# Graph attention on one Trainium2 core: the source-term rows, the maxima, the out-degrees and the second load of x change their places

## The chip, the cores and the metric

The kernel runs on one core of a Trainium2 chip. The metric is the device time of one execution in microseconds (us): from the runs, the median. Five engines work beside each other: TensorE (PE; its weight loads are PEld), VectorE (DVE), ScalarE (ACT), GpSimd (POOL) and SyncE (SP, which only issues transfers here). DMAs are issued by SP and by POOL; each of the two has a queue of its own.

## What is computed

Two layers on 1250 nodes with 1024 features and 20000 edges; each step adds to x. The first step is the graph attention that this change is about:

```python
z = jnp.einsum('ni,hif->nhf', h, W)            # h = layernorm(x); 4 heads of 256
el = jnp.einsum('nhf,hf->nh', z, a_l)
er = jnp.einsum('nhf,hf->nh', z, a_r)
e = jax.nn.leaky_relu(el[src] + er[dst], 0.2)
m = jax.ops.segment_max(e, dst, num_segments=N)
ex = jnp.exp(e - m[dst])
s = jax.ops.segment_sum(ex, dst, num_segments=N)
out = jax.ops.segment_sum((ex / s[dst])[:, :, None] * z[src], dst, num_segments=N)
```

Then follow a feed-forward step (rails, gelu and one large product), a graph convolution, for which the out-degree of each node (plus one, to the power -1/2) is needed, and a mixture of eight experts. Those three are not touched, but for the place where the out-degrees are made.

## The kernel before

The 1250 nodes are ten tiles of 125 (T = 10, R = 125). The edges become a dense matrix of counts: `count(d)` multiplies one-hot matrices of the edges on PE for the destinations of tile d, and `finish` writes the counts to DRAM (`cnt_d`, for the graph convolution), a mask `nm_d` (-1e30 where there is no edge) to DRAM too, and the transposed counts as 16-bit integers to `CT`, which stays in SBUF.

The four heads go in two pairs, g = 0 and 1. `z_weights(g)` loads the weights of a pair; `z_tile(g, t)` multiplies on PE (L131), copies the result to `Z` on ACT (L132), and makes the pair's `el` and `er` of the tile with four VectorE instructions (L136). The counting stage holds all of the first pair's z between the counts (L225 to L240). Then comes a branch (L242, L243): were the edges not sorted as expected, all counts would be made anew. The branch holds every engine, and what lies in it can't be mixed with other work.

Behind the branch, for a pair:

- `maxima(g)` needs `el` of the pair as two rows on all 125 partitions. `to_rows` (L107 to L115) makes them: transpose on PE, copy on ACT (L112), a DMA of 9.8 KB to a row in DRAM (L114) and a second one, 1220.7 KB, that spreads the row to all partitions (L115), both on POOL's queue. Then for each tile d a mask of 125 x 1250 is loaded from `nm_d` on SP's queue (two DMAs, L45 and L46; two buffers), and one VectorE instruction a head (L264) adds mask and row and keeps the maximum: 20 of them for a pair. `maxima` is a generator: it gives control back after each, so that its caller can put other work between.
- `bounds(g)` makes two small tables from the maxima (L272 to L278) and has `to_rows` spread them, one head after the other, as `rows[h]` (two buffers for four heads).
- `attend(h, b)` does head h for half b of the destinations in ten steps: L317 on VectorE, an exponential on ACT (L318), L321 on VectorE (times the counts), five matmuls on PE (L323). Then five results are divided and added to `X` (L327 to L331). So `X`, a second copy of x that collects the sums, must be there at the end of the first pass. u and w have three buffers. After each step it may draw one piece from a generator given to it (`between`).

The order as it is written (L284 to L366): `maxima(0)` is drawn two at a time behind each tile of the second pair's z; bounds(0); the out-degrees `dis` (ten sums over `CT`, L298, then L299 to L301); the second load of x into `X` (ten tiles, two DMAs each, on SP's queue, L305); then, with `maxima(1)` drawn one a step, the passes (0,0), (0,1), (1,0); bounds(1); then (1,1), (2,0), (3,0), (2,1), (3,1).

The program is written with a layer that sets the semaphores and places the buffers. When it builds the program it may move an instruction ahead of others of its engine that are written earlier, if its inputs and its buffer are free. So the file's order is a wish, and the trace shows what became of it: L298 stands behind the first pair's maxima in the file and starts at 246.6 us, while the first maximum starts at 265.4; of the ten tiles of the second pair's z, two are copied out before the branch (at 234.7 and 241.6 us) and eight behind it. A buffer of a pool that reuses another pool's space waits until that is released; the pool `mx0` of the first pair's maxima takes space of the counting stage.

Of the kernel before, what the change touches and what calls it, by code (L numbers as in the profile page):

```python
# [20 lines left out]
R, T = 125, 10  # L21
# [16 lines left out]
def gnn_ffn_kernel(ctx, tc, x, src, dst, gat_w, a_l, a_r, maker, up, cproj,  # L38
# [65 lines left out]
    el, er, mx, el2, el8 = (zp.tile([R, H, T], F32, name=n) for n in ("el", "er", "mx", "el2", "el8"))  # L104
    xT = xTp.tile([P, KD, N], F32, name="xT")

    def to_rows(pool, psp, dst_t, cols, k, n):  # L107

        pt = psp.tile([P, 4, R], F32, name="pt")
        nc.tensor.transpose(pt[:k, 0, :], cols, ident[:R, :R])  # L110
        st = pool.tile([k, R], F32, name=f"st{k}", bufs=1)
        nc.scalar.copy(st, pt[:k, 0, :])  # L112
        row = dram.tile([k, R], F32, name=f"row{n}")
        nc.gpsimd.dma_start(row, st)  # L114
        nc.gpsimd.dma_start(dst_t, row.rearrange("k r -> (k r)").partition_broadcast(R))  # L115

    with tc.tile_pool(name="gw", bufs=1) as gwp, tc.tile_pool(name="gps", bufs=3, space=PSUM) as psp:
# [10 lines left out]
        def z_tile(g, t):  # L128
            pz = psp.tile([R, 2, F], F32, name="pz", bufs=2)
            for k in range(KD):  # L130
                nc.tensor.matmul(pz, xT[:, k, t * R:(t + 1) * R], W[g][:, k], start=(k == 0), stop=(k == KD - 1))  # L131
            nc.scalar.copy(Z[:, t, 2 * g:2 * g + 2, :F], pz)  # L132
            for h in (2 * g, 2 * g + 1):
                for i, e in enumerate((el, er)):
                    sc = gwp.tile([R, F], F32, name="sc", bufs=2)
                    nc.vector.scalar_tensor_tensor(sc, Z[:, t, h, :F], 1.0, aw[g][:, i, h - 2 * g, :], op0=ALU.mult,  # L136
                                                   op1=ALU.mult, accum_out=e[:, h, t:t + 1])

        with tc.tile_pool(name="cc", bufs=1) as ccp, tc.tile_pool(name="cw", bufs=2) as cwp:
# [102 lines left out]
            elsewhere = nc.values_load(flag[0:1, 0:1], min_val=0, max_val=1)  # L242
            with tc.If(elsewhere > 0):  # L243
# [7 lines left out]
                                                 start=(c == 0), stop=(c == EC - 1))  # L251
                        finish(d, pc)

        def maxima(g, mxp, psp):

            el_row = mxp.tile([R, 2, N], F32, name="el_row")
            to_rows(mxp, psp, el_row.rearrange("p a n -> p (a n)"), el[:, 2 * g:2 * g + 2, :].rearrange("p h t -> p (h t)"),
                    2 * T, f"el{g}")
            for d in range(T):
                nm = mxp.tile([R, N], F32, name="nm2", bufs=2)  # L260
                dma(nc.sync, nm, nm_d[d])
                for h in (2 * g, 2 * g + 1):
                    sc = mxp.tile([R, N], F32, name="sc2")
                    nc.vector.tensor_tensor_reduce(sc, nm, el_row[:, h - 2 * g, :], scale=1.0, scalar=-3.0e38,  # L264
                                                   op0=ALU.add, op1=ALU.max, accum_out=mx[:, h, d:d + 1])
                    yield

        def bounds(g, pool, psp, rowp):

            hs = slice(2 * g, 2 * g + 2)  # L270
            for dst_t, f in ((el2, SLOPE), (el8, 1.0 - SLOPE)):
                nc.vector.tensor_scalar(dst_t[:, hs], el[:, hs], f, None, op0=ALU.mult)  # L272
            top = pool.tile([R, 2, T], F32, name="top")
            nc.vector.tensor_tensor(top, mx[:, hs], er[:, hs], op=ALU.add)
            nc.vector.scalar_tensor_tensor(top, top, SLOPE, top, op0=ALU.mult, op1=ALU.max)
            bd = pool.tile([R, 2, 2, T], F32, name="bd")
            nc.vector.tensor_tensor(bd[:, :, 0], er[:, hs], top, op=ALU.subtract)
            nc.vector.scalar_tensor_tensor(bd[:, :, 1], er[:, hs], SLOPE, top, op0=ALU.mult, op1=ALU.subtract)  # L278
            for h in range(2):
                rows[2 * g + h] = rowp.tile([R, 2, N], F32, name="rr", bufs=2)  # L280
                to_rows(pool, psp, rows[2 * g + h].rearrange("p a n -> p (a n)"), bd[:, h].rearrange("p a t -> p (a t)"),
                        2 * T, f"bd{2 * g + h}")

        rows = {}  # L284
        rowst = ExitStack()
        rowp = rowst.enter_context(tc.tile_pool(name="rowp", bufs=1, side="right"))
        with tc.tile_pool(name="mx0", bufs=1) as mxp:
            search = maxima(0, mxp, psp)
            for t in range(T):
                z_tile(1, t)  # L290
                next(search)
                next(search)
            for _ in search:
                pass
            bounds(0, mxp, psp, rowp)

            for t in range(T):
                nc.vector.tensor_reduce(dis[:, t:t + 1], CT[:, t, :], AX.X, ALU.add)  # L298
            nc.vector.tensor_scalar(dis, dis, 1.0, None, op0=ALU.add)  # L299
            nc.scalar.activation(dis, dis, AF.Sqrt)  # L300
            nc.vector.reciprocal(dis, dis)  # L301

    X = ctx.enter_context(tc.tile_pool(name="xpool", bufs=1)).tile([R, T, D], F32, name="X")
    for t in range(T):
        dma(nc.sync, X[:, t, :], x_t[t])  # L305
    HN = N // 2
    HT = T // 2
    norm = {}
    with tc.tile_pool(name="att", bufs=3) as atp, tc.tile_pool(name="aps", bufs=6, space=PSUM) as aps, \
# [21 lines left out]
                nc.vector.scalar_tensor_tensor(xs, po[i][:, :F], rs, xs, op0=ALU.mult, op1=ALU.add)  # L331

        with tc.tile_pool(name="mx1", bufs=1) as mxp:
            search = maxima(1, mxp, tps)
            for h, b in ((0, 0), (0, 1), (1, 0)):
                attend(h, b, search)
            for _ in search:
                pass
            bounds(1, mxp, tps, rowp)
            attend(1, 1)  # L340
        xT = xTp.tile([P, KD, N], F32, name="xT")
        with tc.tile_pool(name="al", bufs=2) as lnp:
            attend(2, 0)
# [517 lines left out]
```

## Time and profile before

| what | value |
|---|---|
| time, median of 3 runs | 3266.51 us (3264.94 to 3267.15) |
| the profiled execution's own time | 3264.68 us |
| its span, first to last instruction | 3263.0 us |
| its mean granted PE clock | 0.987 |
| maxima L264, both pairs | 40, 1.46 us each, from 265.4 to 405.7 us |
| out-degree sums L298 | 10, 1.45 us each, from 246.6 to 279.2 us |
| spread of a source row, second pair | 19.4 us from issue to landing |
| spread of a bounds row | 4, 7.8 to 8.0 us from issue to landing |
| second load of x | 20 DMAs on SP's queue, issued from 322.9 to 350.3 us |
| one attention matmul L323 | 800 records, mean 394 ns |

The profile is of one execution, so places in it are given in us from its first instruction. A busy time is what an engine's instructions took; two neighbouring ones overlap a little, so a row of equal instructions is better counted from start to start. What is named behind an idle time is the event that came last before the engine went on. Transfers are listed with the time from issue to landing. An instruction of a float32 matmul appears as two records.

### The profile page before, as it was taken

What the parts mean: (1) busy time and instruction counts of PE and PEld (TensorE: products, weight loads), DVE (VectorE), ACT (ScalarE), POOL (GpSimd) and SP (SyncE); (2) the same over time, 40 slices, a digit from 0 to 9 for tenths busy, and PEclk for the clock granted to TensorE, in tenths of its full rate; (3) what the DMA queues carried; (4) which work ended last, traced back from release to release, by engine and by line L of the source; (5) the groups of instructions that cost most, each with busy time, mean ns of one, the idle gap of its engine ahead of it and who ended that gap; (6) DMA issues with size and microseconds to landing.
All of it is one profiled execution on the core that took longest, in us unless ns stands there. A gap on an engine that the chain in (4) does not pass through costs nothing. (4 is left out here: it accounts for less than half of the span.)

```text
span 3263.0 us, 23844 instructions
## 1 busy us (share of the span) xinstructions
PE 3159.9 (97%) x9330; PEld 1552.0 (48%) x9330; DVE 1641.6 (50%) x2621; ACT 354.8 (11%) x470; POOL 128.9 (4%) x202
## 2 busy tenths in 40 slices
PE   8996798999999999999999999999999899999998
PEld 5572686444444444444444444444444344445674
DVE  6567897555555555555555555554555720211113
ACT  1211234000000100000010000001000011000000
POOL 1000000000000000000000000000000000001001
PEclk9998898999999999999999999999999999999999
DMA  4245511101110110111011011101110201213564
GB/s 116 59 110 133 146 32 55 39 27 33 39 33 27 40 39 27 33 39 33 27 37 42 27 33 36 37 27 33 40 31 13 77 5 39 70 41 103 182 211 152
DMA packets 104961, 189.76 MB, mean 58 GB/s; under 512 B 32713, under 2 KB 51245, under 8 KB 104088
## 3 DMA queue, kind: packets, MB, share of 16 engines
q1 hardware_dynamic: 95158, 161.26, 16.6%
q0 software_dynamic: 9680, 26.85, 2.9%
q8 instruction: 78, 1.28, 0.2%
q14 instruction: 45, 0.37, 0.0%
HBM read 156.86 MB, written 31.21 MB: 58 GB/s over the span
## 5 line engine op out<-in xcount | busy, mean ns | idle before, releaser
L484 PE MATMUL po<-B,gt 128*125 128x512 f32 x1920 | 836.0, 593 | 0.0
L489 DVE TENSOR_TENSOR acc<-po,acc 125x512 f32<-125x512 f32 x620 | 425.9, 690 | 486.1 <-PE po L484 483.0
L484 PEld LDWEIGHTS po<-B,gt 128*125 128x125 f32 x1920 | 360.7, 188 | 465.0 <-issue 457.0
L484 PE MATMUL po<-t,s 128*125 128x512 f32 x1280 | 559.8, 592 | 0.0
L484 PEld LDWEIGHTS po<-t,s 128*125 128x125 f32 x1280 | 237.9, 188 | 294.1 <-issue 293.6
L495 DVE TENSOR_TENSOR X<-po,X 125x512 f32<-125x512 f32 x320 | 220.8, 690 | 262.3 <-PE po L484 262.3
L484 PE MATMUL po<-B,s 128*125 128x512 f32 x640 | 299.5, 607 | 0.0
L484 PE MATMUL po<-t,gt 128*125 128x512 f32 x640 | 280.4, 592 | 2.8 <-DVE X L493 2.3
L438 ACT ACTIVATE gt<-pz 128x1668 f32<-128x1668 f32 (+1 forms) x96 | 149.8, 1560 | 688.8 <-PE pz L436 688.8
L323 PE MATMUL po<-Z,w 125*125 125x257 f32 x800 | 187.1, 394 | 30.6 <-DVE w L321 16.8
L484 PEld LDWEIGHTS po<-t,gt 128*125 128x125 f32 x640 | 119.9, 188 | 158.0 <-issue 145.9
L484 PEld LDWEIGHTS po<-B,s 128*125 128x125 f32 x640 | 112.5, 187 | 165.4 <-issue 108.9
L323 PEld LDWEIGHTS po<-Z,w 125*125 125x125 f32 x800 | 152.9, 195 | 63.0 <-DVE w L321 29.6
L634 PE MATMUL ph<-Hs,cs 125*125 125x512 f32 x400 | 173.5, 593 | 0.0
L493 DVE TENSOR_TENSOR X<-X,po 125x512 f32<-125x512 f32 x160 | 109.5, 686 | 120.1 <-PE po L484 120.1
L131 PE MATMUL pz<-W,xT 128*125 128x512 f32 x320 | 141.4, 596 | 3.7 <-ACT Z L132 3.7
L574 PE MATMUL ph<-W,xT 128*125 128x512 f32 x320 | 140.1, 596 | 0.0
L427 ACT COPY pw<-pz 128x128 f32<-128x128 f32 x32 | 8.5, 265 | 1131.7 <-PE pz L424 1131.7
L216 PE MATMUL pc<-os,od 125*125 125x417 f16 (+1 forms) x642 | 119.2, 343 | 1.0 <-DVE od L187 1.0
L634 PEld LDWEIGHTS ph<-Hs,cs 125*125 125x125 f32 x400 | 74.3, 188 | 93.1 <-issue 93.1
L665 PE MATMUL pab<-xgT,w 128*128 128x256 f32 x512 | 112.0, 379 | 1.4 <-DVE xgT L762 1.4
L665 PEld LDWEIGHTS pab<-xgT,w 128*128 128x128 f32 x512 | 96.6, 190 | 15.5 <-DVE xgT L762 1.9
(181 smaller groups left out, 2104.3 us busy)
## 6 DMA issues: line engine op xcount, KB each, us to landing
B<-in_cproj SPq DMA_DIRECT2D x128, 512.0 KB, 3.8
w<-in_w SPq DMA_DIRECT2D x16, 1024.0 KB, 8.1
nm<-nm_d SPq DMA_DIRECT2D x20, 546.9 KB, 4.4
w3t<-in_w SPq DMA_DIRECT2D x8, 1024.0 KB, 7.0
ys_d<-y SPq DMA_DIRECT2D x16, 512.0 KB, 5.3
cnt_d<-cn SPq DMA_DIRECT2D x10, 546.9 KB, 6.3
nm_d<-nm SPq DMA_DIRECT2D x10, 546.9 KB, 6.1
cs<-cnt_d SPq DMA_DIRECT2D x10, 546.9 KB, 4.2
```

Source lines behind the costliest of these rows:

```text
L131: nc.tensor.matmul(pz, xT[:, k, t * R:(t + 1) * R], W[g][:, k], start=(k == 0), stop=(k == KD - 1))
L216: nc.tensor.matmul(pc[:, b, :nn], od[:, d - near[c][0], :], os[:, n0:n0 + nn], start=(c == win[d][0]), stop=(c == win[d][-1]))
L323: nc.tensor.matmul(po[i], w[:, i * R:(i + 1) * R], Z[:, s, h, :], start=(s == 0), stop=(s == T - 1))
L427: nc.scalar.copy(pw[b], pp[:, 0, :P])
L438: nc.scalar.activation(gt[b][:, :, n0:n0 + nn], pz[:, :, :nn], AF.Gelu)
L484: nc.tensor.matmul(po, a[:, k, n * R:(n + 1) * R], w[:, k, :], start=(k == 0), stop=(k == 1))
L489: tt(acc[m][:, n, :], po, acc[m][:, n, :], op=ALU.add)
L493: tt(x, x, po, op=ALU.subtract)
L495: tt(x, po, x, op=ALU.add)
L574: nc.tensor.matmul(ph[:, g, :], xT[:, k, t * R:(t + 1) * R], W[:, k, g * 512:(g + 1) * 512], start=(k == 0), stop=(k == KD - 1))
L634: nc.tensor.matmul(pa[:, g, :], cs[:, c, :], Hs[:, c, g * 512:(g + 1) * 512], start=(c == late_first[0]), stop=(c == late_first[-1]))
L665: nc.tensor.matmul(pab[:, :nn], w12[:, i, k, f * P:(f + 1) * P], rhs[:, k, n0:n0 + nn], start=(k == 0), stop=(k == KD - 1))
```

## The change

Several steps are moved; no arithmetic changes.

- `to_rows` is split: `to_row` writes the row to DRAM, `spread` brings it to all partitions. `el_row(g, ...)` is `to_row` for the source terms of a pair.
- The first pair's source row is written ahead of the branch, from a pool of the counting stage; behind it, `maxima(0)` has only to spread it. The masks get three buffers for the first pair (two for the second, as before).
- The first pair's maxima are drawn three at a time ahead of each tile of the second pair's z, so all 20 are drawn by the seventh tile.
- The second load of x goes to POOL's queue, where it stands behind the bounds' rows.
- The second pair's source row is written ahead of the pass (0,0), but spread, and its maxima drawn, only from the pass (0,1) on.
- The out-degrees become a generator, one sum a step, that the pass (1,1) draws.

```diff
-    def to_rows(pool, psp, dst_t, cols, k, n):
+    def to_row(pool, psp, cols, k, n):
...
         row = dram.tile([k, R], F32, name=f"row{n}")
         nc.gpsimd.dma_start(row, st)
+        return row
+
+    def el_row(g, pool, psp):
+        return to_row(pool, psp, el[:, 2 * g:2 * g + 2, :].rearrange("p h t -> p (h t)"), 2 * T, f"el{g}")
+
+    def spread(dst_t, row):
+
         nc.gpsimd.dma_start(dst_t, row.rearrange("k r -> (k r)").partition_broadcast(R))
...
+            row0 = el_row(0, cwp, psp)
 
             elsewhere = nc.values_load(flag[0:1, 0:1], min_val=0, max_val=1)
...
-        def maxima(g, mxp, psp):
+        def maxima(g, mxp, row):
 
-            el_row = mxp.tile([R, 2, N], F32, name="el_row")
-            to_rows(mxp, psp, el_row.rearrange("p a n -> p (a n)"), el[:, 2 * g:2 * g + 2, :].rearrange("p h t -> p (h t)"),
-                    2 * T, f"el{g}")
+            els = mxp.tile([R, 2, N], F32, name="els")
+            spread(els.rearrange("p a n -> p (a n)"), row)
             for d in range(T):
-                nm = mxp.tile([R, N], F32, name="nm2", bufs=2)
+                nm = mxp.tile([R, N], F32, name="nm2", bufs=3 - g)
...
         with tc.tile_pool(name="mx0", bufs=1) as mxp:
-            search = maxima(0, mxp, psp)
+            search = maxima(0, mxp, row0)
             for t in range(T):
+                for _ in range(3):
+                    next(search, None)
                 z_tile(1, t)
-                next(search)
-                next(search)
-            for _ in search:
-                pass
             bounds(0, mxp, psp, rowp)
-
-            for t in range(T):
-                nc.vector.tensor_reduce(dis[:, t:t + 1], CT[:, t, :], AX.X, ALU.add)
-            nc.vector.tensor_scalar(dis, dis, 1.0, None, op0=ALU.add)
-            nc.scalar.activation(dis, dis, AF.Sqrt)
-            nc.vector.reciprocal(dis, dis)
...
     for t in range(T):
-        dma(nc.sync, X[:, t, :], x_t[t])
+        dma(nc.gpsimd, X[:, t, :], x_t[t])
...
-            search = maxima(1, mxp, tps)
-            for h, b in ((0, 0), (0, 1), (1, 0)):
-                attend(h, b, search)
-            for _ in search:
-                pass
+            def degrees():
+
+                for t in range(T):
+                    nc.vector.tensor_reduce(dis[:, t:t + 1], CT[:, t, :], AX.X, ALU.add)
+                    if t == T - 1:
+                        nc.vector.tensor_scalar(dis, dis, 1.0, None, op0=ALU.add)
+                        nc.scalar.activation(dis, dis, AF.Sqrt)
+                        nc.vector.reciprocal(dis, dis)
+                    yield
+
+            row1 = el_row(1, mxp, tps)
+            attend(0, 0)
+            search = maxima(1, mxp, row1)
+            attend(0, 1, search)
+            attend(1, 0, search)
             bounds(1, mxp, tps, rowp)
-            attend(1, 1)
+            attend(1, 1, degrees())
```

More of the change, by code (lines that the diff above doesn't have):

```diff
@@ L263, in maxima @@
                     sc = mxp.tile([R, N], F32, name="sc2")
-                    nc.vector.tensor_tensor_reduce(sc, nm, el_row[:, h - 2 * g, :], scale=1.0, scalar=-3.0e38,
+                    nc.vector.tensor_tensor_reduce(sc, nm, els[:, h - 2 * g, :], scale=1.0, scalar=-3.0e38,
                                                    op0=ALU.add, op1=ALU.max, accum_out=mx[:, h, d:d + 1])
@@ L280, in bounds @@
                 rows[2 * g + h] = rowp.tile([R, 2, N], F32, name="rr", bufs=2)
-                to_rows(pool, psp, rows[2 * g + h].rearrange("p a n -> p (a n)"), bd[:, h].rearrange("p a t -> p (a t)"),
-                        2 * T, f"bd{2 * g + h}")
+                spread(rows[2 * g + h].rearrange("p a n -> p (a n)"),
+                       to_row(pool, psp, bd[:, h].rearrange("p a t -> p (a t)"), 2 * T, f"bd{2 * g + h}"))
         rows = {}
```

## The prediction

> **What bounds the kernel now.** I read the page's busy table first, then the windows around the change, then the timeline inside them.
>
> ```profile
> PE 3159.9 (97%) x9330; PEld 1552.0 (48%) x9330; DVE 1641.6 (50%) x2621; ACT 354.8 (11%) x470; POOL 128.9 (4%) x202
> ```
>
> TensorE (PE) is the bound of the program as a whole, so only its idle time can be won. The windows from the branch (244) to the last attention pass (515) show where that is. Columns: window, its length, then busy time (and instructions) of PE, PEld, DVE, ACT and POOL, granted clock, DMA share, GB/s.
>
> ```profile
> 244.00:258.00 14.00, 13.70 (x34) 5.90 (x33) 9.65 (x14) 1.43 (x3) 1.04 (x2) 1.00 0.76 196
> 258.00:301.00 43.00, 39.27 (x91) 16.65 (x90) 34.40 (x77) 2.93 (x6) 0.00 (x0) 1.00 0.46 124
> 301.00:326.00 25.00, 0.98 (x4) 0.22 (x3) 13.13 (x37) 4.63 (x8) 3.11 (x6) 0.59 0.41 107
> 326.00:420.00 94.00, 76.08 (x303) 60.93 (x304) 82.06 (x143) 25.39 (x33) 0.00 (x0) 0.87 0.51 128
> 420.00:515.00 95.00, 93.39 (x446) 78.86 (x445) 87.22 (x169) 40.76 (x56) 2.07 (x4) 1.00 0.11 27
> ```
>
> PE is idle for 3.7 us in the second, 24.0 in the third, 17.9 in the fourth, 1.6 in the last: with 0.3 in the first some 47 us, all that this change can reach. The timeline says why (start, duration, engine, line; idle before and its releaser in brackets).
>
> ```profile
> 246.61 2.82 DVE L298 TENSOR_REDUCE dis<-CT 125x1 f32<-125x1250 int16 x2 [2.96 <-DVEq L243]
> 247.22 0.51 POOL L114 DMA_DIRECT2D rowel<-st  x1 [74.90 <-ACT st L112]
> 251.84 0.53 POOL L115 DMA_DIRECT2D el_row<-rowel  x1 [4.11 <-DMA rowel<-st]
> 265.44 1.46 DVE L264 CUSTOM_DVE_ANT_0 sc<-nm,el_row 125x1250 f32<-125x1250 f32 x1 [9.19 <-issue]
> ...
> 286.29 0.21 ACT L300 ACTIVATE dis<-dis 125x10 f32<-125x10 f32 x1 [16.11 <-DVE dis L299]
> 287.03 14.00 PE L131 MATMUL pz<-W,xT 128*125 128x512 f32 x32 [3.73 <-ACT Z L132]
> ...
> 310.68 0.25 DVE L272 TENSOR_SCALAR el<-el 125x20 f32<-125x20 f32 x2
> 312.62 0.51 POOL L114 DMA_DIRECT2D rowbd<-st  x1 [60.25 <-ACT st L112]
> 314.49 0.53 POOL L115 DMA_DIRECT2D rr<-rowbd  x1 [1.36 <-DMA rowbd<-st]
> 322.89 2.43 DVE L317 SCALAR_TENSOR_TENSOR u<-rr,el 125x625 f32<-125x625 f32 x3 [11.37 <-DMA rowbd<-st]
> 326.09 10.58 PE L323 MATMUL po<-Z,w 125*125 125x257 f32 x40 [11.10 <-DMA X<-in_x]
> 342.92 1.46 DVE L264 CUSTOM_DVE_ANT_0 sc<-nm,el_row 125x1250 f32<-125x1250 f32 x1 [10.91 <-DMA el_row<-rowel]
> 345.17 16.05 PE L323 MATMUL po<-Z,w 125*125 125x257 f32 x62 [8.49 <-DVE w L321]
> ```
>
> The chain after the branch: row to DRAM, spread to all partitions, 20 maxima from 265.4 to 310.7, bounds, row, spread, 322.9 first attention step, 326.1 first matmul. PE's z product is over at 301. Then the second pair's row arrives at 342.9, after 19.4 us of DMA, and VectorE stands 10.9 us before it with the weights of the next steps queued behind. From there on VectorE is the bound (362 to 420: it is nearly always busy). The order on an engine isn't the file's: L298 is written after all maxima and runs first, L272 of the first pair runs at 176.8, before the branch. Ready instructions are moved up.
>
> [...] a row of 9.8 KB behind a spread on POOL's queue landed after 7.6 us; a spread took 7.8 to 8.0 us alone and 19.4 beside the loads of x on SP's. [...] at 168 to 174 VectorE was busy throughout and POOL's weight loads went out each 0.72 us, with 270 to 337 GB/s moving. [...] clock 0.50 at 314 to 328, and an attention matmul of 0.22 us pitch takes up to 0.79 us there; so each long gap costs about 2 us more.
>
> **The change, part by part.** Durations are of the profiled execution (span 3263.0, time 3264.68); its time is 1.8 us under the median 3266.51, so I add 1.8 at the end.
>
> *Row ahead of the branch.* One PE transpose (0.27), one copy (0.26), one 9.8 KB DMA. All first-pair scores are there at 167.4, so they go into the counting stage; 0.3 us on PE there, 0.3 less behind the branch: nothing. The spread can then be issued with the first load after the branch, at 246.7 instead of 251.8: 5.1 us. It now shares the DMA engines with five tiles of 0.61 MB (three buffers for the first pair, and two that the second pair already fetches now at 248.7) instead of four. At half of the 250 GB/s of that stretch its 1.25 MB need 10 us from 248.5: 259. Bounds: 257[...], 266 if it lands with all 4.3 MB. I take 259, against 265.4 now.
>
> *Maxima ahead of z.* 20 x 1.38 (step to step) = 27.6. Of the eight groups of four score products (4 x 0.345 = 1.38), two come before 259; about four more come before the end of the maxima, 5.5. Waits for nm as now 1.1; the third buffer can take these away. Two out-degree sums caught between, 2.7. End: 259 + 27.6 + 5.5 + 1.1 + 2.7 = 296, against 310.7. The score products behind a waiting maximum hold nobody but the second pair's row: ScalarE's copy L132 frees z's PSUM. From there the same chain as now, 310.7 to 322.9 = 12.2: first step at t0 = 308 instead of 322.9, **15 us earlier**. Bounds: 20 (no sums between, row at 257) and 2 (row at 266, all groups and four sums). The end of z (297 without the 3.7 us that ScalarE's root L300 costs) isn't late then.
>
> *Out-degrees later.* 10 x 1.37 = 13.7 on VectorE, one root, one reciprocal. They read only CT, so nothing ties them to the last pass of this stage; by what L298 does now I expect some five in the wait for the spread row, two as above, the rest in the 11 us wait for the bounds' rows: nothing beyond the 2.7. If they stay where written: an attention pass has 22.0 us of PE and about 18.6 of VectorE (18.2 of 21 and 19.2 of 22 in two quiet windows), cover 3.4, so 10.3 us lost; the root among exponentials adds up to two table loads of 1.28 (as at 322.7) on ScalarE, which is mostly idle. Bounds 0 and 10.3; I take 0.
>
> *Second load of x on POOL's queue.* 20 issues of about 0.53 leave SP, whose nm loads no longer stand behind them, and stand on POOL between the bounds' rows and the second source row. First spread lands at t0, second at t0 + 8, x (5.12 MB at about 250 GB/s) at t0 + 28. The first pass needs half of x at its end, t0 + 27: it landed at about t0 + 18; free. The second source row's spread comes last: t0 + 36. If the 9.8 KB row itself falls behind x, some 3 to 5 more.
>
> *Second pair's maxima from the second pass on.* 27.6 us of VectorE come onto two passes (37.2) instead of three. First pass: 3.2 to first matmul, 22.0, cold clock 2: over at t0 + 27. VectorE has then done three or four steps of the next and waits for t0 + 36, about 9 us (10.9 now). From there 37.2 + 27.6 less 7 done = 58, so the second bounds at about t0 + 92 with the last sums of that pass behind them; now 413.05 - 322.89 = t0 + 90.2. **2 us lost**; bounds: 4 gained if the row doesn't hold it (t0 + 86), 8 lost with a late row.
>
> Sum: 15 - 2 = 13 us. 3264.7 - 13 = 3251.7, with 1.8: **3253**. Everything after 420 shifts as it is.
>
> **The rivals.**
> - *All hidden* (3242): row at 257, no sums between, the second row in time: 20 + 4 = 24. For it: VectorE has idle time to put sums in, as 258 to 265 shows. [...]
> - *Washed out* (3264): 15 is halved to 8 by a late row or sums between the maxima, and the rest goes to the late second row (6 to 8) or to sums that stay in their pass. For it: the 10.9 us wait now; 18.6 + 13.7 is over 22.0.
> - *Slower* (3281): x on POOL's queue is slow. At 150 GB/s it needs 34 us, the row behind it 4 and the spread 8: the second row lands at t0 + 54, 18 later than taken, all of it VectorE wait in the stretch where VectorE is the bound; and the sums, with no gap left, stay in place: 15 - 20 - 10 = -15. It decides from a landing at t0 + 49 on if the sums cost nothing, t0 + 39 if they cost 10. [...] Against: 270 to 337 GB/s of POOL's loads under a busy VectorE.
> - That the order is left as it was can't be excluded, as the builder moves instructions; but row0's buffer is the one thing that held it behind the branch, so this falls under the washed case.
>
> **Numbers.** Likeliest 0.55 (own range 3246 to 3261), all hidden 0.15, washed out 0.17, slower 0.13. About 0.2% (6.5 us) is what a measurement of this kernel can tell from no change. Faster: 0.15 + 0.52 = 0.67; within: 0.17 + 0.03 = 0.20; slower 0.13. The range 3241 to 3271 leaves out the slower case and the outermost of the first rival.
>
> **What would show it.** The row el0 written before 244 and its spread issued near 247; the first maximum near 259, bounds near 296, first attention step near 308; PE's gap before it some 13 us instead of 25; L298's ten sums mostly before 310; the second row landing near 36 us after the first step, VectorE waiting about 9 for it. I am wrong if the first maximum is still at 265, if x lands later than 30 us after the first step, or if the sums stand in the fourth pass and PE idles 10 there.

## The result, and the profile after

| | before | after |
|---|---|---|
| time, median of 6 runs | 3266.81 us (3260.42 to 3268.26) | 3249.52 us (3247.97 to 3255.61) |
| ratio | 1 | 0.9953, 95% interval 0.994 to 0.9965 |
| the profiled execution's own time | 3264.68 us | 3250.55 us |
| its span | 3263.0 us | 3248.8 us |

The changed kernel is faster by 17.3 us in the medians and by 14.1 us between the two profiled executions; the forecast was 3253. Where these 14.1 us lie is read from the same places as before. First the page's busy table of the changed kernel:

```profile
PE 3156.3 (97%) x9330; PEld 1550.1 (48%) x9330; DVE 1642.0 (51%) x2621; ACT 354.8 (11%) x470; POOL 140.7 (4%) x222
```

PE, DVE and ACT run as many instructions as before; POOL has gained the 20 loads of x. The windows of the changed kernel, cut where the old ones were cut by event (end of z, first attention step, the pass (1,1), the last pass; same columns):

```profile
244.00:258.00 14.00, 13.85 (x33) 5.82 (x32) 6.67 (x12) 1.17 (x2) 0.53 (x1) 1.00 0.67 155
258.00:301.00 43.00, 39.99 (x94) 17.21 (x92) 39.10 (x86) 2.93 (x5) 0.00 (x0) 1.00 0.58 154
301.00:322.00 21.00, 0.96 (x3) 0.22 (x3) 11.42 (x35) 4.37 (x9) 4.40 (x9) 0.50 0.34 82
322.00:410.00 88.00, 75.78 (x302) 60.31 (x302) 81.43 (x142) 24.39 (x31) 9.51 (x19) 0.91 0.55 139
410.00:505.00 95.00, 93.15 (x442) 78.72 (x443) 88.55 (x167) 42.05 (x57) 1.79 (x4) 1.00 0.12 27
```

PE is idle for 20.0 us in the third window (24.0 before) and for 12.2 in the fourth (17.9 before). So the gap ahead of the attention, which should have shrunk to some 13, is nearly all there, and the attention passes, which should have lost 2, have won. The timeline of the changed kernel, all engines, shows why:

```profile
247.81 5.54 DVE L336 TENSOR_REDUCE dis<-CT 125x1 f32<-125x1250 int16 x4 [3.02 <-DVEq L251]
248.44 0.53 POOL L122 DMA_DIRECT2D els<-rowel  x1 [13.82 <-DVEq L251]
261.90 1.46 DVE L271 CUSTOM_DVE_ANT_0 sc<-nm,els 125x1250 f32<-125x1250 f32 x1 [8.20 <-DMA nm<-nm_d]
...
301.57 0.18 DVE L281 TENSOR_TENSOR top<-mx,er 125x20 f32<-125x20 f32 x1
301.66 1.45 DVE L336 TENSOR_REDUCE dis<-CT 125x1 f32<-125x1250 int16 x1
303.02 0.17 DVE L282 SCALAR_TENSOR_TENSOR top<-top 125x20 f32<-125x20 f32 x1
304.58 0.18 DVE L285 SCALAR_TENSOR_TENSOR bd<-er,top 125x20 f32<-125x20 f32 x1
304.67 2.81 DVE L336 TENSOR_REDUCE dis<-CT 125x1 f32<-125x1250 int16 x2
304.86 0.57 PE L110 MATMUL pt<-ident,bd 125*20 125x125 f32 x2 [6.87 <-issue]
307.73 0.21 ACT L339 ACTIVATE dis<-dis 125x10 f32<-125x10 f32 x1 [15.98 <-DVE dis L338]
307.85 0.57 ACT L139 COPY Z<-pz 125x512 f32<-125x512 f32 x1
308.35 0.25 ACT L112 COPY st<-pt 20x125 f32<-20x125 f32 x1
308.89 0.51 POOL L114 DMA_DIRECT2D rowbd<-st  x1 [59.91 <-ACT st L112]
...
319.09 2.43 DVE L316 SCALAR_TENSOR_TENSOR u<-rr,el 125x625 f32<-125x625 f32 x3 [9.01 <-DMA rowbd<-st]
...
342.90 0.53 POOL L122 DMA_DIRECT2D els<-rowel  x1 [1.02 <-DMA X<-in_x]
...
360.20 1.45 DVE L271 CUSTOM_DVE_ANT_0 sc<-nm,els 125x1250 f32<-125x1250 f32 x1
```

`top` (L281) is the first instruction that needs all 20 maxima, so its start is the end of the maxima: 301.57, against 310.84 before, 9.3 us won. But the bounds' row is issued at 308.89, against 312.62, and the first attention step starts at 319.09, against 322.89: only 3.8 are left. Between 301.57 and 308.89 lie a sum between L281 and L282, two more sums, and on ScalarE the root (L339), which had been placed ahead of the copy of the row: the transposes were over at 304.86 + 0.57 = 305.4, and the copy L112 started at 308.35.

The first maximum (261.90) needs the spread row and a mask. The view names the mask (`nm<-nm_d`) behind its 8.20 us of waiting, but both transfers of that mask had landed by 253.0. The row landed at 261.09; VectorE then went through seven more waits for semaphores, some 0.1 us each, whose events had come long before. In all nine kernels here that spread the row behind the branch the first maximum starts 0.6 to 0.8 us after the row's landing. So it is the row that it waits for.

VectorE's list of waits in the changed kernel (240 to 530 us) has none for the second pair's row any more. The two longest single waits are these (in total, times, longest; the second is the one just explained):

```profile
DVE u L316 <- DMA rowbd<-st: 9.0, 1, 9.0
DVE sc L271 <- DMA nm<-nm_d: 8.2, 1, 8.2
```

The second row was issued at 342.90 and took 11.8 us, to 354.7, but the first maximum that reads it stands at 360.20, behind the eighth `w` (L320) of the pass (0,1), and doesn't wait. PE's own list shows its first 47 us of attention in one piece, where before it had stood still for 8.49 us ahead of 345.17:

```profile
322.30 47.42 PE L322 MATMUL po<-Z,w 125*125 125x257 f32 x202 [11.03 <-DVE w L320]
```

The attention from its first matmul to the first of the pass (1,1) takes 87.9 us (322.30 to 410.24) instead of 93.9 (326.09 to 419.95). The last pass starts at 504.61 instead of 514.20: **9.6 us** earlier, 3.8 from the start and 5.9 from the passes (rounded).

From there the program is the same, and yet the span's end is another 4.6 us nearer. That isn't the change but the clock that PE was granted. PE transposes in the feed-forward step, with a window of that place (columns as above, the clock third from the end), of before and then of after:

```profile
547.51 1.87 PE L90 MATMUL pt<-ident,xn 125*128 125x125 f32 x8
551.00 1.93 PE L90 MATMUL pt<-ident,xn 125*128 125x125 f32 x8
546.00:556.00 10.00, 9.33 (x31) 6.07 (x30) 2.80 (x7) 3.90 (x10) 2.23 (x6) 0.50 0.50 166
```

```profile
537.62 1.02 PE L90 MATMUL pt<-ident,xn 125*128 125x125 f32 x8
539.46 1.07 PE L90 MATMUL pt<-ident,xn 125*128 125x125 f32 x8
536.00:546.00 10.00, 6.69 (x38) 3.94 (x36) 6.67 (x11) 7.42 (x13) 4.19 (x6) 0.97 0.54 181
```

The same eight took nearly twice as long in the one execution. PE had been idle for 6.24 us ahead of this place in both; after that the clock stayed at half for 23.9 us in the one and for 6.8 us in the other. Matched one by one, PE's instructions stand at the same distance from the start of the last pass up to this gap, to within 0.01 us; within 30 us behind it a difference of 5.4 us has come up, and it stays for some 1900 us (0.7 are given back towards the end). Of the eleven kernels profiled here five show the long form and five the short one, whichever way they were changed, and the time from the last pass to the end of the span goes with it: 2747 to 2749 us with the long form, 2742 to 2745 with the short one, 2746.4 in the one kernel that begins with the long and goes on with the short (e1). A single profile carries some 5 us of this, and even a median of few runs does. In 35 runs beside four of the experiments the kernel before took 3257.6 to 3262.8 us 15 times and 3264.1 to 3268.1 us 20 times; group against group (3260.4 against some 3249, some 3267 against 3255.6) the change is worth some 11 of the 17.3 us, an estimate, and by the start of the last pass 9.6. That is why the experiments below are read from the start of the first step and of the last pass first, and from the time second.

### The profile page after: what moved, and what is told of

It reads as the page before. It is cut to its first block, busy times and chain, and to the rows that moved or that the text cites. A ratio compares the mean times of both kernels' runs of the same rounds, so it can differ in the third digit from the quotient of the medians.

```text
span 3248.8 us, 23843 instructions
## 1 busy us (share of the span) xinstructions
PE 3156.3 (97%) x9330; PEld 1550.1 (48%) x9330; DVE 1642.0 (51%) x2621; ACT 354.8 (11%) x470; POOL 140.7 (4%) x222
## 3 DMA queue, kind: packets, MB, share of 16 engines
q8 instruction: 78, 1.28, 0.2%
## 4 chain that ended last, share of the span: by engine, by line
PE 85%; DVE 3%; issue 2%; DMA 1%; ACT 0%; POOL 0%; DVEq 0%; POOLq 0%; SPq 0%; ACTq 0%
PE po L493 59%; PE pab L674 5%; PE ph L643 5%; PE ph L583 4%; PE po L322 4%; PE pz L445 3%; PE po L778 2%; PE pt L90 1%; PE po L789 1%; DVE sc L271 1%; PE pg L629 1%; DVE w L320 0%; DVE u L316 0%; DVE st L76 0%; DVE y L781 0%
```

## Experiments

The theory after seeing this (A): the chain from the branch to the first step is now held by the out-degree sums and their root, which the builder moves in there; and the passes won because x on POOL's queue puts off the second pair's maxima until their row is there. The rivals: the spread of the row and the masks set the first step whatever else stands there (B); the later start of the second maxima was won by the written order alone (C). Each was run beside the kernel before, and the ratio is to those runs. The places, in us, are of one profiled execution each; "passes" is from the first attention matmul to that of the pass (1,1).

| kernel | median us | ratio to before, 95% | first maximum | `top` | first step | passes | last pass |
|---|---|---|---|---|---|---|---|
| before | 3266.81 | 1 | 265.44 | 310.84 | 322.89 | 93.9 | 514.20 |
| after | 3249.52 | 0.9953 (0.994 to 0.9965) | 261.90 | 301.57 | 319.09 | 87.9 | 504.61 |
| e1_no_sums | 3242.07 | 0.9928 (0.9915 to 0.9942) | 263.65 | 299.54 | 311.49 | 86.8 | 495.61 |
| e2_sums_pinned | 3253.72 | 0.9969 (0.9958 to 0.998) | 263.05 | 298.94 | 310.96 | 87.7 | 507.88 |
| e3_sums_first | 3244.41 | 0.9934 (0.992 to 0.9947) | 263.65 | 301.14 | 313.37 | 87.0 | 497.68 |
| e9_root_later | 3247.9 | 0.995 (0.9936 to 0.9963) | 263.10 | 302.78 | 317.36 | 86.8 | 501.69 |
| e5_x_on_sp | 3258.31 | 0.9975 (0.9965 to 0.9986) | 262.90 | 302.57 | 319.98 | 91.0 | 508.36 |
| e6_first_pair_alone | 3260.31 | 0.9988 (0.9982 to 0.9994) | 262.89 | 302.55 | 319.91 | 93.1 | 510.48 |
| e7_row_alone | 3264.46 | 1.0 (0.9991 to 1.001) | 262.65 | 308.93 | 322.36 | 93.8 | 513.61 |
| e8_spread_ahead | 3236.56 | 0.992 (0.9907 to 0.9933) | 254.12 | 290.02 | 301.98 | 88.6 | 490.18 |
| e8b_spread_ahead_3 | 3246.14 | 0.9942 (0.993 to 0.9954) | 253.51 | 289.41 | 308.76 | 87.5 | 495.68 |

**e1_no_sums: the changed kernel without the out-degrees.** It leaves the sums and the root out and sets `dis` to a constant, so its output isn't the network's.

```diff
-            def degrees():
...
-            attend(1, 1, degrees())
+            attend(1, 1)
...
+    nc.vector.memset(dis, 0.25)
```

> This kernel leaves the out-degrees out (dis is a constant), all else as in the changed kernel. Theory A: four of the ten sums stand between the first pair's maxima, one and a root stand in the bounds' chain, and ScalarE's copy of the bounds' row waits behind that root (5.4 us from the transposes' end at 305.4 to the copy's end included); without them the first attention step comes 9 to 10 us earlier than 319.1 and the time falls by as much, to about 3240. Rival B: only the sums' own 4 x 1.37 count, the chain is set by the row that lands at 261 and by z: about 5 us less, 3244 to 3245.

Measured: 3242.07 us; the first step at 311.49, 7.6 us earlier than in the changed kernel, although its first maximum came 1.75 us later. The maxima took 35.9 us (263.65 to 299.54) instead of 39.7, and from `top` to the first step it was 12.0 us (17.5). What follows: the sums and their root cost 3.8 us among the maxima and 5.5 behind them, so B falls as it was put and A's chain is shown. (Three sums stood among the maxima, not the four that were expected here, and from the transposes' end to the end of the row's copy it had been 3.2 us, not 5.4.) But the row keeps its part: it landed at 262.93 here, 1.8 us later than in the changed kernel, and the first maximum followed it. That is why 7.6 us were won and not 9 to 10.

**e2_sums_pinned: the sums held in the pass where they are written.** An edge in the order keeps each sum behind the `u` of its step.

```diff
-                    nc.vector.tensor_reduce(dis[:, t:t + 1], CT[:, t, :], AX.X, ALU.add)
+                    with tc.issue_after(first["u"].ins):
+                        nc.vector.tensor_reduce(dis[:, t:t + 1], CT[:, t, :], AX.X, ALU.add)
```

> The sums are held in the pass (1,1), where the change wrote them, each behind that step's first VectorE instruction. Theory A: 9 to 10 us won before the first step as without the sums, and about 10 lost in the pass (1,1), where 13.7 us meet a cover of 3.4: the same as the changed kernel within 2 us, PE idle some 10 us in that pass. Rival B: 5 won, 10 lost, about 5 us slower than the changed kernel.

Measured: 3253.72 us. The first step came at 310.96, 8.1 us earlier than in the changed kernel, but the last pass 3.3 us later. PE in the pass (1,1):

```profile
401.89 1.97 PE L324 MATMUL po<-Z,w 125*125 125x257 f32 x8 [0.99 <-DVE w L322]
...
411.81 2.43 PE L324 MATMUL po<-Z,w 125*125 125x257 f32 x10 [0.43 <-DVE w L322]
414.67 2.43 PE L324 MATMUL po<-Z,w 125*125 125x257 f32 x10 [0.43 <-DVE w L322]
...
434.12 6.04 PE L324 MATMUL po<-Z,w 125*125 125x257 f32 x19 [2.72 <-DVE w L322]
```

PE waits behind each step's five products (ten records): from start to start a step takes 2.86 us, where ten steps of this pass take 21.8 in the changed kernel. The pass took 32.2 us (401.89 to 434.12), 10.5 more, and the next pass another 1.2. The last wait, 2.72 us, is longer than those of the steps ahead of it, 0.43 each. The root is there: on VectorE the add ahead of it starts at 428.84 and the reciprocal behind it at 430.70. So some 2.3 of the 10.5 (2.72 less 0.43, an estimate) are put down to the root and its table loads, which took 2.8 us together in e9. What follows: the 9 to 10 us that theory A expected ahead of the first step came nearly whole (8.1), against the rival's 5; in one pass there isn't room for ten sums and the root; the written order, had it been kept, would have been worse than what the builder made of it, by 3.3 us at the last pass.

**e3_sums_first: the sums and the root right behind the branch, ahead of the maxima.**

```diff
+            for t in range(T):
+                nc.vector.tensor_reduce(dis[:, t:t + 1], CT[:, t, :], AX.X, ALU.add)
...
             search = maxima(0, mxp, row0)
...
-            attend(1, 1, degrees())
+            attend(1, 1)
```

> The sums and their root stand right behind the branch, ahead of the first pair's maxima. Ten sums from 247.8 on end at about 261.5, where the first maximum begins now (261.9). Theory A: as without the sums, first attention step near 310, about 3240. Rival B: at most 5 us won; if the row would land earlier without the wait for VectorE, nothing.

Measured: 3244.41 us, 5.1 less than the changed kernel. VectorE behind the branch:

```profile
247.12 13.71 DVE L296 TENSOR_REDUCE dis<-CT 125x1 f32<-125x1250 int16 x10 [2.95 <-DVEq L251]
263.65 1.46 DVE L271 CUSTOM_DVE_ANT_0 sc<-nm,els 125x1250 f32<-125x1250 f32 x1 [2.82 <-DMA nm<-nm_d]
```

All ten fit ahead of the first maximum, which waits another 2.82 us. (The view names a mask again; the row landed at 262.83.) So the wait for the spread row has room for the ten sums; the changed kernel puts four there and leaves it idle for 8.2 us. The first step is at 313.37, 5.7 us earlier: less than theory A's 310, as the row landed 1.7 us later than in the changed kernel and the maxima took 1.6 us more than without the sums.

**e9_root_later: the changed kernel with only the end of the out-degrees held back.**

```diff
-                        nc.vector.tensor_scalar(dis, dis, 1.0, None, op0=ALU.add)
+                        with tc.issue_after(first["u"].ins):
+                            nc.vector.tensor_scalar(dis, dis, 1.0, None, op0=ALU.add)
                         nc.scalar.activation(dis, dis, AF.Sqrt)
```

> The changed kernel with only the end of the out-degrees held back: the add behind the ten sums gets an edge that keeps it behind the steps of the pass (1,1) written before it, so the root on ScalarE and the reciprocal come there too; the ten sums stay free to move. Theory A: in the changed kernel the root stood ahead of the z copy and of the bounds' row's copy on ScalarE and held both for about 2.9 us (the row's transposes were over at 305.4, the copy started at 308.35). Without it the bounds' row is issued near 306.0 instead of 308.9, the first attention step is near 316.2 instead of 319.1 and the time near 3246.5 (3 us less), less up to 1.3 for a table load between the exponentials that nobody waits for. Rival B: VectorE's two sums behind the bounds or PE's order hold the row, not ScalarE: first step within 1 us of 319.1, time near 3249.5.

Measured: 3247.9 us, which the intervals can't tell from the changed kernel. The trace can, with all engines of this kernel around the bounds:

```profile
305.79 0.17 DVE L285 SCALAR_TENSOR_TENSOR bd<-er,top 125x20 f32<-125x20 f32 x1
305.88 2.81 DVE L338 TENSOR_REDUCE dis<-CT 125x1 f32<-125x1250 int16 x2
306.06 0.57 PE L110 MATMUL pt<-ident,bd 125*20 125x125 f32 x2 [8.30 <-issue]
306.59 0.25 ACT L112 COPY st<-pt 20x125 f32<-20x125 f32 x1 [8.21 <-PE pt L110]
307.13 0.51 POOL L114 DMA_DIRECT2D rowbd<-st  x1 [58.24 <-ACT st L112]
```

From L285 to the row's DMA it is now 1.34 us; in the changed kernel it was 4.31 (304.58 to 308.89). The two sums stand at the same place, so they weren't what held it: the root on ScalarE was, for 3.0 us. From `top` to the first step it is 14.6 us, 2.9 less than in the changed kernel; the maxima happened to end 1.2 later, so the first step is 1.7 earlier, and the last pass 2.9. Theory A holds; B falls. The rest of the 17.5 - 12.0 = 5.5, 2.6 us, is the sum and the score products between L281 and L285.

**e5_x_on_sp: the second load of x back on SP's queue.**

```diff
-        dma(nc.gpsimd, X[:, t, :], x_t[t])
+        dma(nc.sync, X[:, t, :], x_t[t])
```

> The second load of x goes back to SP's queue, all else as in the changed kernel. Theory A: the place of x on POOL's queue is what let the second pair's maxima slip behind the landing of their row; with x on SP they are drawn from the first pass's end on again and VectorE waits some 10 us for a row that lands 19 us after its issue: 4 to 6 us slower than the changed kernel, about 3255. Rival B: it is the writing of the maxima one pass later that helped, the queue doesn't matter: the same as the changed kernel within 2 us.

Measured: 3258.31 us, 8.8 more than the changed kernel; the first step 0.9 later, the passes 91.0 (3.1 longer), the last pass 3.8 later. VectorE's longest wait in this kernel's passes:

```profile
DVE sc L271 <- DMA els<-rowel: 9.3, 1, 9.3
```

It is the wait that the prediction expected of the changed kernel. On SP's queue the loads of x begin at 320.44, beside the second row's spread (issued at 320.64), which then takes 18.3 us (11.8 in the changed kernel), and the builder puts the first maximum behind the fourth `w` (L320) of the pass (0,0), where it waits until 339.01 and holds the weights `w` behind it. What follows: the written order alone (C) doesn't account for the passes; x on POOL's queue is worth 3 to 4 us at the last pass, and it works through the order that the builder chooses, more than through the row's landing: the row lands at 354.7 there and at 339.0 here. The medians differ by more than the last pass does; the clock in the feed-forward step can account for some 5 us of such a difference, but these runs don't tell how much of it.

**e6_first_pair_alone: the same, and the second pair's maxima from the first pass on, as before.**

```diff
-        dma(nc.gpsimd, X[:, t, :], x_t[t])
+        dma(nc.sync, X[:, t, :], x_t[t])
...
-            attend(0, 0)
             search = maxima(1, mxp, row1)
+            attend(0, 0, search)
             attend(0, 1, search)
             attend(1, 0, search)
+            for _ in search:
+                pass
```

> The changed kernel with the second pair as before: x on SP's queue and the second pair's maxima drawn from the first pass on. Theory A: first attention step near 319.5 as in the changed kernel, then the passes as in the kernel before, 94 us from the first matmul to the pass (1,1) with VectorE waiting about 10 us for the second row: 4 us faster than before, about 3262. Rival B (the first pair's part carries most of the gain): 10 us or more faster than before.

Measured: 3260.31 us; the first step at 319.91 and the passes at 93.1, as before the change; the last pass 3.7 earlier than before, as theory A had it (4), not the rival's 10. What follows: the part of the change ahead of the attention is worth 3 to 4 us alone. With x on SP's queue the second-pass start of the maxima brings 2.1 (93.1 to 91.0), and x on POOL's queue 3.1 more. So C holds for about a third of the 5.9 that the passes won, in this order of steps; x on POOL's queue with the maxima from the first pass on wasn't run.

**e7_row_alone: the kernel before with the source rows written ahead, and nothing else.**

```diff
+            row0 = el_row(0, cwp, psp)
...
-            search = maxima(0, mxp, psp)
+            search = maxima(0, mxp, row0)
...
+            row1 = el_row(1, mxp, tps)
-            search = maxima(1, mxp, tps)
+            search = maxima(1, mxp, row1)
```

> The kernel before with one part of the change alone: the first pair's row is written ahead of the branch. Theory A (the row's landing beside the mask loads, and the sums that are moved between the maxima, set the first step): spread issued near 248 instead of 251.8, first maximum near 261, first attention step near 319, the passes as before; about 4 us faster than before. Rival B (the row's DRAM round trip was the wait): the full 5 us of the round trip won at the first maximum and at the first step, 317 to 318.

Measured: 3264.46 us, no change that can be told. VectorE in this kernel:

```profile
262.65 1.46 DVE L271 CUSTOM_DVE_ANT_0 sc<-nm,els 125x1250 f32<-125x1250 f32 x1 [9.66 <-DMA nm<-nm_d]
...
285.71 1.45 DVE L305 TENSOR_REDUCE dis<-CT 125x1 f32<-125x1250 int16 x1
287.08 1.45 DVE L271 CUSTOM_DVE_ANT_0 sc<-nm,els 125x1250 f32<-125x1250 f32 x1
288.46 1.45 DVE L305 TENSOR_REDUCE dis<-CT 125x1 f32<-125x1250 int16 x1
```

The first maximum is 2.8 us earlier, with the row (261.84; 264.83 before), but the maxima are stretched to 46.3 us (45.4 before): they are drawn two a tile of z, and sums stand between. The first step is 0.5 earlier, so both expectations, 4 and 5 us, missed. The row ahead brings next to nothing alone. That it takes maxima drawn earlier to make use of it is likely; maxima drawn earlier without the row were not run.

**e8_spread_ahead and e8b_spread_ahead_3: a version of my own.** In both the first pair's row is not only written but spread ahead of the branch, into a buffer that both pairs share; three sums stand right behind the branch, and the other seven are spread over the passes (1,1), (2,0) and (3,0), held there by edges. In e8 all maxima and the bounds are written ahead of the second pair's z; in e8b the maxima are three a tile as in the changed kernel, and the bounds behind z.

```diff
             row0 = el_row(0, cwp, psp)
+            spread(els0.rearrange("p a n -> p (a n)"), row0)
...
+            for t in range(3):
+                nc.vector.tensor_reduce(dis[:, t:t + 1], CT[:, t, :], AX.X, ALU.add)
...
+            for _ in search:
+                pass
+            bounds(0, mxp, psp, rowp)
             for t in range(T):
-                for _ in range(3):
-                    next(search, None)
                 z_tile(1, t)
-            bounds(0, mxp, psp, rowp)
...
-            attend(1, 1, degrees())
+            attend(1, 1, degrees((3, 4), 3))
```

> A version of its own: the first row is spread ahead of the branch as well, into a buffer both pairs share; three out-degree sums right behind the branch, the other seven shared out over three later passes; all maxima of the first pair written ahead of z. Theory A: first maximum when the first mask has landed, near 254; 20 maxima and the score products between them end near 290, first attention step near 302 to 304, 15 us ahead of the changed kernel; sums in the later passes nearly covered; about 3236, if the second row isn't later by more than a few us for standing behind x. Rival B: z, over at 298, and the release of its PSUM hold the first step at 310 or later; about 3242.

> As the version before it, but with the first pair's maxima three ahead of each z tile as in the change; here the second pair's small row is issued ahead of x on POOL's queue, there behind it. Theory A: first step as there; the second row lands some 4 us earlier, so equal or up to 4 us faster; about 3235. Rival B: the same as the version before it within 2 us, as VectorE doesn't wait for that row.

Measured: e8 3236.56 us, 13 less than the changed kernel and 0.992 of the kernel before (0.9907 to 0.9933): it **beats both**, and comes close to what was expected of it (about 3236, first step 302 to 304). e8b is 3246.14. In both, the spread is issued near 238, ahead of the branch, instead of 248.4, and has landed by 247.6. So the first maximum, near 254, no longer waits for the row, and the maxima end at 289.4 to 290.0. Against the changed kernel, e8's first step is 17.1 us earlier: 7.8 at the first maximum, 3.8 among the maxima (no sums there) and 5.6 behind them (no sum and no root there). Of these, 14.4 are left at the last pass, as the seven sums in the later passes cost some. e8 and e8b differ in PE's order behind the maxima. e8, then e8b:

```profile
290.81 0.37 PE L110 MATMUL pt<-ident,bd 125*20 125x125 f32 x2 [0.48 <-PE pz L138]
291.03 7.89 PE L138 MATMUL pz<-W,xT 128*125 128x512 f32 x18
...
291.78 0.51 POOL L114 DMA_DIRECT2D rowbd<-st  x1 [52.67 <-ACT st L112]
...
301.98 2.43 DVE L323 SCALAR_TENSOR_TENSOR u<-rr,el 125x625 f32<-125x625 f32 x3 [0.94 <-DMA rowbd<-st]
```

```profile
285.77 11.75 PE L138 MATMUL pz<-W,xT 128*125 128x512 f32 x27
297.36 0.38 PE L110 MATMUL pt<-ident,bd 125*20 125x125 f32 x2
298.72 0.51 POOL L114 DMA_DIRECT2D rowbd<-st  x1 [60.31 <-ACT st L112]
...
308.76 2.43 DVE L323 SCALAR_TENSOR_TENSOR u<-rr,el 125x625 f32<-125x625 f32 x3 [8.94 <-DMA rowbd<-st]
```

In e8 the bounds' transposes, written ahead of z, cut into z, and the row is on its way while z still runs. In e8b the bounds are ready on VectorE at 290.1 (L288 at 289.93), yet PE takes the transposes only when z is over: 7 us, all of it found again at the first step (6.8 later) and 5.5 of it at the last pass. (The medians are 9.6 apart; the half clock ahead of the feed-forward step is long in the profile of e8b and short in that of e8.) e8b had been expected to be no slower; that fell, and what e8's rival named, z holding the first step near 310, is what happened in e8b. Once the row is early enough, the order on PE is the next limit.

## Why the prediction was right or wrong

The time was forecast well, and largely by luck, as errors cancelled: of the 13 us expected, the first step should have given 15 and the passes taken 2; the first step gave 3.8 and the passes gave 5.9. Another 4.6 of the 14.1 between the two profiled executions are the clock's and no part of the change.

- **The row ahead of the branch** was right in kind: its spread was issued 0.5 us after the first load behind the branch, at 248.44 for 246.7; the branch itself came 1 us later than in the execution before. The size was off: the spread took 12.6 us, to 261.09, where 10 were taken, although three tiles of masks moved beside it and not five. (In the kernel before it had taken 13.0, to 264.83.) In these 12.6 us 222 GB/s were moving, and the row's 1.25 MB make 99 of them, not half of 250. With 0.8 us of semaphore waits behind the landing, the first maximum came at 261.90 instead of 259, inside the bounds given (257 to 266): 2.9 us of the miss.
- **The maxima** took 39.7 us instead of the 37 of the sum. Three out-degree sums stand among them, not two (1.4 more), and 23 score products, not 16 (2.4 more); the waits for masks (1.1 in the sum) are gone. 2.7 us of the miss.
- **"From there the same chain as now, 12.2"**: this step failed. With no sum or root behind the maxima the chain is 12.0 (e1, e2, e8), so the price was right, but not what stands in it: 17.5. A sum and the score products between L281 and L285 cost 2.6, the root ahead of the copy of the row 2.9 (e9). 5.5 us of the miss; together 2.9 + 2.7 + 5.5 = 11.1, which is all that lies between 308 and 319.09.
- **"Out-degrees: nothing beyond the 2.7"** is the same failure seen from the step's side. Taken away they give 7.6 us at the first step (e1). The prediction saw that sums would be drawn up into waits, and put "the rest in the 11 us wait for the bounds' rows". But three of the ten stood ahead of that wait, between the last maximum and the row's DMA, and the root with them. Its upper bound, 10.3 in the pass (1,1), was right to a few tenths for that pass in the order as written (10.5 in e2), though there the root, which it put at nothing, had some 2.3 of it. What wasn't asked was who waits behind a root on ScalarE: in the kernel before it had cost a 3.73 us stall of PE among z, and the prediction counted on that stall's going without asking where the root would stand next. In the changed kernel ScalarE stood 15.98 us ahead of the root, whose input came at 307.69, and two copies stood behind it: that of a z product that was over at 298.0 started at 307.85, and that of the row, whose transposes were over at 305.4, at 308.35.
- **x on POOL's queue** was right in its numbers: the second row landed at 354.7, 35.6 us after the first step, for 36. The loads of x were over 30.9 us after it, for 28; "later than 30" had been named as a sign of being wrong, and did no harm, as no step of VectorE or PE waited for x.
- **"VectorE waits for t0 + 36, about 9 us"** failed, in the other direction. That wait exists where x is on SP's queue (9.3 us in e5, 9.9 in e6), and was assumed to stay. The builder put the first maximum of the second pair behind the eighth `w` of the pass (0,1), at t0 + 41, where the row had been there for 5.5 us. So the second bounds began at t0 + 87.1, inside the bounds given (86 to 98), where t0 + 92 was taken and t0 + 90.2 was before. These are 3.1 of the 5.9 us that the passes won instead of losing 2. The other 2.8 come behind the bounds, which the prediction took as the end of the matter: PE, which had not stood still for 8.49 us, had 4.1 us of work left from there to the pass (1,1), and 6.9 before.
- **"Each long gap costs about 2 us more"** was right for the kernel before, though it sets a pitch (0.22 us) beside a duration (0.79): at half clock the pitch is 0.43 (327.11 to 327.54), and as the half clock reached 3.4 us into the attention, 1.7 were lost. In the changed kernel it reached 6.1 us into it (322.30 to 328.36), which makes 3.0.
- **Everything after shifts as it is**: right for the work, but the first products of the feed-forward step stand 5.4 us apart in the two profiled executions, and the ends of the spans 4.6, in work that no part of the change touches. Behind the same gap of 6.24 us the clock was at half for 23.9 us in the one and for 6.8 us in the other, and the same eight transposes took 1.93 and 1.07 us. What sets how long it lasts, no run shows.
- **The rivals.** "All hidden" failed on the sums, "washed out" came nearest for the first step (3.8 instead of its 8), but didn't have the won wait. The slower case didn't occur: the second row landed at t0 + 35.6, far from its t0 + 54.

What stays open: why the builder sets the second pair's first maximum later when x is on POOL's queue. The traces show it without exception (behind 18 or 19 `w`s in the seven kernels with x there, behind 4 in the four with x on SP's queue), but it was not taken apart.

## What to carry to other kernels

When a step is moved to "where it costs nothing", follow each of its instructions to the engine it ends on and ask what stands behind it in that queue: a root of 0.2 us held the row that all waited for by 3 us. If a chain is to be shortened, pin the rest out of it or put it where a wait is sure (ten sums fit behind the branch), and write what must go first on every engine of the chain, PE too, ahead of the long work. Take the event that a view names behind a wait as a hint and compare it with the landing times: here a mask was named, and the row was waited for. And read what a change is worth from the start of the stage behind it, since one profile against another can carry some 5 us of the clock.

## What the runs showed that was not expected

GpSimd didn't issue its loads in one go. Seven loads of x went out from 320.18 to 323.9, about 0.53 us each; the eighth waited 3.88 us until a bounds row's spread that was issued before them had landed, and the later ones went out two by two, each pair when an earlier load had landed, with 7.3 us of waiting in six places:

```profile
323.34 0.54 POOL L45 DMA_DIRECT2D X<-in_x  x1
327.77 0.52 POOL L46 DMA_DIRECT2D X<-in_x  x1 [3.88 <-DMA rr<-rowbd]
329.71 0.54 POOL L45 DMA_DIRECT2D X<-in_x  x1 [1.43 <-DMA X<-in_x]
```

The eighth load stands for the same reason in e8 (4.28 us) and e9 (4.11 us). So the second row behind x was held not only on its way (11.8 us from issue to landing; the four bounds rows took 7.8 to 8.3) but at its issue, 342.90, which is 19.6 us after the seventh load. The traces' semaphores say what sets this limit: the program gives POOL's transfers eight semaphores in turn (110 to 117), and each transfer waits for the one issued eight places ahead of it, which had the same semaphore. The eighth load comes eight places behind the bounds row's spread. So it is the program's limit here, eight transfers open at a time; what the chip itself would hold, no run shows.

The half clock ahead of the feed-forward step came in pieces: its stretches there lasted 3.4, 6.8, 10.2, 23.9 or 27.3 us in the eleven traces, which are whole multiples of 3.41 (the shortest stretch in the records of the kernel before and of the changed one is 3.413 us). It set in 2.3 to 3.6 us after PE's last attention matmul in the five kernels with the short form, and sooner (2.2) or later (4.1 to 5.2) in the five with the long one. That is seen in eleven executions and was not steered.

The prediction had put a switch of ScalarE's tables at up to two loads of 1.28 us. In e9, where the root falls among the exponentials, it is just that: loads at 420.08 and at 421.61, the exponential at 422.90, 2.8 us in all with the root, and the pass took 21.8 us as in the changed kernel. From the first load's start to the root's it was 1.30 us. In e2, where the root comes at the end of the pass, PE stood 2.72 us there.
